# A scatter that waits for the scatter two places ahead of it, in a routed-experts kernel

## The chip, the cores and the metric

The kernel runs on one core of one Trainium2 chip. The metric is the device time of one execution in microseconds; three executions of the kernel before were timed, and their median is what the prediction is compared with. One more execution was recorded by the hardware profiler; every duration of a single instruction below comes from that recording.

The engines are called as in the profile: PE (matmuls), PEld (its weight loads), DVE (vector), ACT (scalar), POOL (GpSimd) and SP (which here only starts DMAs). SPq, POOLq and so on are the engines' queues.

## The reference

The input `x` has 16 rows of 512 tokens with 128 features. Each token is normalised to `xn`, and the result is

```
x + attention(xn) + experts(xn)
```

The attention is linear, with a decay: `scores[t, s] = (q[t]·k[s]) * d**(s-t-1)` for `s > t`, no softmax, with 32 features in q, k and v. The experts are four feed-forward networks; a router takes the two largest of four logits for each token, and only the two chosen results count:

```
logits = xn @ router_w + router_b + load_balancer
rw, sel = top_k(logits, 2);  rw = softmax(rw)
e0 = (silu(xn @ w1) * (xn @ w3)) @ w2          e1 = gelu(linear(xn) @ c1w + c1b) @ c2w + c2b
e2 = two layer norms around a relu network      e3 = gelu(xn @ ml_w1 + ml_b1) @ ml_w2 + ml_b2
out = x + attention + rw[0] * e_sel0 + rw[1] * e_sel1
```

All data are 32-bit floats.

## The kernel before

**First part: rows.** The 16 rows are loaded, normalised, transposed and projected. Four rows at a time (a "quad") go through the attention, are added to `x`, and are stored to the output by a plain DMA on SP. The rows are also gathered in six groups of 1, 1, 2, 4, 4 and 4 rows for the routing. For a group, `route` and `count` on DVE work out which pair of experts each token wants and which place in that pair's list it gets; there are six pairs, so six lists, all in one DRAM table called `lists`. Then the group's normalised tokens are written to their places. That is `Group.send`, one indirect DMA for each 128 tokens, issued by POOL. Each row of it has 131 floats: 128 features, two weights and the token's number, which lie in SBUF in a tile called `pay`. The places lie in a tile called `idx`, one column for each scatter. There are 64 such list scatters, named `send0.0` to `send5.15` in the plan.

**Second part: tiles.** The lists are read back in 21 tiles of two to four times 128 tokens (`TURN` gives the order: pair, number, and the group that must have been sent). A tile is loaded from `lists` into `xg` by SP (step `L`), transposed (`T`), pushed through the two experts of its pair, and summed in `o`: step `B` on DVE puts the biases into `o`, and the steps `J` on DVE add the experts' results. Then `Tile.send` adds `o` to the output, again by one indirect DMA for each 128 tokens, this time with accumulation in DRAM; the steps are called `X0` to `X3`. There are 66 of these output scatters. Their token numbers lie in a tile `to`, one column for each. There are four buffers for `o`, so `B` of a tile waits until the scatters of the tile four places ahead have landed.

**The order.** Each step is given to `add` with its engine, an estimated duration, the steps it follows, the buffers it takes and a rank. `emit` is a list scheduler over these: it keeps a time for each engine (`free`), works out when each ready step could start, picks the step that starts first (or a lower rank within 0.25 us of it), and calls its function, which writes the instructions. The order in which the functions are called is then the order on each engine, for PE, DVE, ACT and SP by a manual schedule, and for POOL by `queued`, which chains the instructions one behind the other. POOL is `G` in the plan. It has three kinds of work: the scatters, the powers `rstd_x`, `rstd_u` and `rstd_v` of the norms (`inverse`), and small copies and memsets.

Both kinds of scatter go through the helper `scatter`:

```
i = queued(nc.gpsimd.indirect_dma_start(
    out=o, out_offset=bass.IndirectOffsetOnAxis(ap=index, axis=0),
    in_=src, in_offset=None, bounds_check=n - 1, oob_is_err=False, **how,
), key)
```

In the plan a list scatter is a step of 1.28 us on POOL and an output scatter one of 1.87 us. Scatters post their completion to eight semaphores in turn, so before the change a scatter waits at most for the one eight places ahead of it.

At the very end there is a loop over rows that runs only if a list overflowed; it does not run with these inputs.

Of the kernel before, what the change touches and what calls it, by code (L numbers as in the profile page):

```python
# [83 lines left out]
def decay_attention__plus__routed_experts(  # L84
# [10 lines left out]
    nc = tc.nc  # L95
# [17 lines left out]
        "h2T": 1, "z2T": 1, "o": 4,  # L113
    }

    LATE = {"x": 3.0, "o": 3.2, "pay1": 2.6, "pay2": 2.6}


# [25 lines left out]
    def queued(i, key=None):  # L144

        if queue["on"]:
            others = [q for q, k in queue["moving"] if k != key or key is None]
            for q in others or [queue["fixed"]]:
                if q is not None:
                    tc.add_manual_dep(i.ins, q, behind, reason="the order of the plan")  # L150
            if key:
                queue["moving"].append((i.ins.name, key))
            else:
                queue.update(fixed=i.ins.name, moving=[])
        return i
# [7 lines left out]
    PE, V, A, G, S = "PVAGS"  # L163
# [7 lines left out]
    def emit():  # L171
        free = dict.fromkeys("PVAGS", 0.0)
        slots = {kind: [()] * n for kind, n in ROOM.items()}
        slots["x"] = [(f"store{b}",) for b in range(ROOM["x"])]
        done, left = {}, {n: len(p[3]) for n, p in plan.items()}
        followers = {}
        for n, p in plan.items():
            for q, _ in p[3]:
                followers.setdefault(q, []).append(n)
        ready = [n for n in plan if not left[n]]  # L180
        while ready:
            starts = {}
            for n in ready:
                eng, us, fn, after, takes, rank, at = plan[n]
                t = max(at, free[eng])
                for q, lat in after:
                    if lat is None:
                        lat = 0.05 if plan[q][0] == eng else 0.2
                    t = max(t, done[q] + lat)
                for kind in {k for k, _ in takes}:  # L190
                    ends = sorted(
                        max((done[q] for q in s), default=-1.0) + LATE.get(kind, 0.2)
                        for s in slots[kind] if all(q in done for q in s)
                    )
                    count = sum(k == kind for k, _ in takes)
                    t = max(t, ends[count - 1]) if len(ends) >= count else None
                    if t is None:
                        break
                if t is not None:
                    starts[n] = t  # L200
            assert starts, f"no step can go on: {ready}"
            first = min(starts, key=starts.get)
            eng, soon = plan[first][0], starts[first] + 0.25
            n = min(
                (m for m in starts if plan[m][0] == eng and starts[m] <= soon),
                key=lambda m: (plan[m][5], starts[m]),
            )
            eng, us, fn, after, takes, rank, at = plan[n]
            for kind, users in takes:
                i = min(  # L210
                    (i for i, s in enumerate(slots[kind]) if all(q in done for q in s)),
                    key=lambda i: max((done[q] for q in slots[kind][i]), default=-1.0),
                )
                slots[kind][i] = (n, *users)
                given.setdefault((kind, n), []).append(i)
            running[0] = n
            fn()
            running[0] = None
            done[n] = free[eng] = starts[n] + us
            ready.remove(n)  # L220
            for m in followers.get(n, ()):
                left[m] -= 1
                if not left[m]:
                    ready.append(m)
        assert len(done) == len(plan), "a step waits for itself"
# [253 lines left out]
    def transposed(z, n, name):  # L479
# [2 lines left out]
            nc.tensor.transpose(pt[:, ts(c, P)], z(c), ident)  # L482
        return pt[:, : n * P]

    def scatter(o, src, index, n, key, **how):

        i = queued(nc.gpsimd.indirect_dma_start(  # L487
            out=o, out_offset=bass.IndirectOffsetOnAxis(ap=index, axis=0),
            in_=src, in_offset=None, bounds_check=n - 1, oob_is_err=False, **how,
        ), key)  # L490
        tc.add_to_no_dep_group(key, i.ins)
        tc.declare_no_dep(i.ins, group=key, reason="each row of the table is written once at most")
        if key == "lists":
            tc.declare_no_dep(i.ins, group="loads", reason="a tile is loaded when all its rows are there")

    def chosen(lg, n, pool, name):

        cin = pool.tile([P, NL, 1 + n], F32, tag=f"cin{n}", name=f"cin_{name}")  # L500
        pair = cin[:, :, 1:]
        dif = pool.tile([P, NL, n], F32, tag=f"dif{n}", name=f"dif_{name}")
        firsts = [(e, NE - 1 - e, e * (2 * NE - 1 - e) // 2) for e in range(NE - 1)]
        for e, m, at in firsts:
            nc.vector.tensor_tensor(
                dif[:, at : at + m], lg[:, e : e + 1].to_broadcast([P, m, n]), lg[:, e + 1 :], ALU.subtract
            )

        won = pool.tile([P, NL, n], F32, tag=f"won{n}", name=f"won_{name}", bufs=1)
        nc.vector.tensor_scalar(won, dif, 0.0, 0.5, ALU.is_ge, ALU.subtract)  # L510

        sums = pool.tile([P, NE, n], F32, tag=f"sums{n}", name=f"sums_{name}", bufs=1)
        w = lambda l: won[:, l, :]
        nc.vector.tensor_tensor(sums[:, 1, :], w(3), w(4), ALU.add)
        nc.vector.tensor_tensor(sums[:, 2, :], w(5), w(3), ALU.subtract)
        nc.vector.scalar_tensor_tensor(sums[:, 3, :], w(4), -1.0, w(5), ALU.mult, ALU.subtract)
        nc.vector.tensor_reduce(sums[:, 0, :], won[:, : NE - 1].rearrange("p l c -> p c l"), AX.X, ALU.add)
        nc.vector.tensor_tensor(sums[:, 1:], sums[:, 1:], won[:, : NE - 1], ALU.subtract)
        for e, m, at in firsts:
            nc.vector.tensor_tensor(  # L520
                pair[:, at : at + m], sums[:, e : e + 1].to_broadcast([P, m, n]), sums[:, e + 1 :], ALU.add
            )
        nc.vector.tensor_scalar(pair, pair, 1.5, None, ALU.is_gt)
        return cin, dif
# [173 lines left out]
    class Group:  # L698
# [52 lines left out]
        def send(s, k):  # L751
            scatter(lists, s.entry(k), s.idx[:, k : k + 1], NL * LR, "lists")
# [30 lines left out]
    for g, m in enumerate(GROUPS):  # L783
# [41 lines left out]
        n = NC * m  # L825
# [19 lines left out]
    class Tile:  # L845
# [138 lines left out]
        def send(s, c):  # L984
            scatter(rows_of_out, s.o[:, c, :], s.to[:, c : c + 1], B * T, "out", compute_op=ALU.add)
# [69 lines left out]
    with tc.manual_schedule(engines={E.PE, E.DVE, E.Activation, E.SP}):  # L1055
        queue["on"] = True
        emit()
        queue["on"] = False
# [29 lines left out]
    with tc.For_i(0, trips, 1) as i:  # L1088
# [20 lines left out]
        s = Dense(0, 3, 0, NC, "row")  # L1109
# [90 lines left out]
```

## Time and profile before

| what | value |
|---|---|
| time, median of 3 | 320.58 us (319.81 to 322.14) |
| time of the profiled execution | 373.55 us |
| span of the profiled execution | 371.5 us |
| granted PE clock in it, mean | 0.891 |
| PE busy | 307.8 us (83%) |
| DVE busy | 208.7 us (56%) |
| POOL busy | 203.6 us (55%) |
| ACT busy | 160.1 us (43%) |
| list scatters on POOL | 64, mean 991 ns |
| output scatters on POOL | 66, mean 1561 ns |

The profiled execution is 53 us longer than the median of the timed ones. Its durations are those of single instructions, and sums of them are compared with its own time. [...] In a timeline line the columns are the start in us, the duration in us, engine, source line and operation, what is written and read, the number of instructions, and in brackets the idle time before with what ended it.

### The profile page before, as it was taken

The page shows a single profiled execution, that of the slowest core. Times are in us where ns is not written, and L with a number is a line of the kernel's source. Part 1 is how long each engine was busy: PE and PEld are TensorE (multiplying, and loading weights), DVE is VectorE, ACT ScalarE, POOL GpSimd, SP SyncE. Part 2 cuts the span into 40 slices and gives each one's busy share as a digit, 9 for nine tenths or more (in the row PEclk, how much of TensorE's full clock was granted, in tenths as well). Part 3 has the DMA queues.
Part 4 walks back from the last instruction along what each step waited for, and adds up shares of the span by engine and source line. Part 5 has one row for each costly group of instructions (what it writes and reads, how often), then busy time and mean ns, then how long its engine had stood idle before and what let it go on. Part 6 is the DMA issues. An engine that isn't in the chain of part 4 may idle for free. (4 is left out here: it accounts for less than half of the span.)

```text
span 371.5 us, 6510 instructions
## 1 busy us (share of the span) xinstructions
PE 307.8 (83%) x2194; PEld 234.0 (63%) x2194; DVE 208.7 (56%) x857; ACT 160.1 (43%) x358; POOL 203.6 (55%) x247
## 2 busy tenths in 40 slices
PE   1996979879300998996999999999999999999970
PEld 1854858455300695865468785775886877885860
DVE  4875657739230385731375964785858685475420
ACT  3784764336200613353253636144476266333420
POOL 5508773744775030277648884844364641784282
PEclk9986886668655599999899999999999999999995
DMA  7991174440251005021505362422133310442032
GB/s 225 283 205 50 39 211 117 119 119 8 78 167 43 1 17 156 9 75 36 79 8 66 28 89 21 66 21 36 12 55 58 43 16 1 69 48 19 3 33 23
DMA packets 34148, 25.60 MB, mean 69 GB/s; under 512 B 3648, under 2 KB 31552, under 8 KB 33984
## 3 DMA queue, kind: packets, MB, share of 16 engines
q0 software_dynamic: 11552, 8.50, 16.6%
q1 hardware_dynamic: 21840, 15.39, 16.4%
q10 hardware_dynamic: 720, 1.26, 1.0%
q8 instruction: 19, 0.31, 0.4%
q14 instruction: 17, 0.14, 0.1%
HBM read 11.65 MB, written 13.62 MB: 68 GB/s over the span
## 5 line engine op out<-in xcount | busy, mean ns | idle before, releaser
L487 POOL DMA_INDIRECT out_dram<-o,to x66 | 103.0, 1561 | 48.2 <-DVE o L939 33.1
L487 POOL DMA_INDIRECT lists<-pay,idx x64 | 63.4, 991 | 48.7 <-DVE sc L637 19.3
L939 DVE SCALAR_TENSOR_TENSOR o<-y_ps,xg,o 128x128 f32<-128x128 f32 x132 | 38.0, 345 | 51.7 <-PE y_ps L158 41.6
L158 PE MATMUL y_ps<-main_sb,h 128*128 128x128 f32 x456 | 55.4, 276 | 0.9 <-ACT h L916 0.9
L158 PEld LDWEIGHTS y_ps<-main_sb,h 128*128 128x128 f32 x456 | 53.7, 192 | 3.7 <-issue 1.2
L158 PE MATMUL proj_ps<-w_all,xnT 128*128 128x68 f32 x128 | 22.6, 344 | 19.3 <-ACT xnT L565 19.2
L158 PEld LDWEIGHTS proj_ps<-w_all,xnT 128*128 128x128 f32 x128 | 21.1, 254 | 21.0 <-ACT xnT L565 20.5
L158 PE MATMUL h_ps<-xT,main_sb 128*128 128x512 f32 (+2 forms) x88 | 34.1, 487 | 0.0
L916 ACT ACTIVATE h<-h_ps,cols_sb 128x512 f32<-128x512 f32 (+2 forms) x44 | 24.7, 579 | 17.2 <-PE h_ps L158 11.9
L902 DVE SCALAR_TENSOR_TENSOR th<-th,a_ps 128x384 f32<-128x384 f32 (+2 forms) x36 | 20.2, 566 | 18.8 <-ACT th L899 18.3
L158 PE MATMUL a_ps<-xT,w_sb 128*128 128x384 f32 (+2 forms) x72 | 29.9, 501 | 0.5 <-ACT xT L867 0.5
L916 ACT ACTIVATE h<-h_ps,b_e 128x512 f32<-128x512 f32 (+2 forms) x28 | 17.4, 626 | 29.7 <-PE h_ps L158 29.4
L158 PE MATMUL b_ps<-xT,w_sb 128*128 128x384 f32 (+2 forms) x72 | 28.5, 525 | 0.4 <-ACT xT L867 0.4
L899 ACT ACTIVATE th<-a_ps 128x384 f32<-128x384 f32 (+2 forms) x36 | 17.8, 499 | 24.9 <-PE a_ps L158 24.4
L475 ACT ACTIVATE pay<-x,off_x,rstd_x 128x128 f32<-128x128 f32 x64 | 26.1, 487 | 2.5 <-DVE off_x L470 2.5
L158 PEld LDWEIGHTS y_ps<-sw_w2h,h 128*128 128x128 f32 x224 | 26.1, 192 | 1.3 <-issue 0.5
L465 POOL TENSOR_TENSOR rstd_x<-ve_x,neg_half 128x4 f32<-128x4 f32 x16 | 16.4, 1030 | 18.9 <-DVE ve_x L460 15.2
L158 PE MATMUL y_ps<-sw_w2h,h 128*128 128x128 f32 x224 | 26.5, 275 | 0.0
L158 PE MATMUL h_ps<-xT,w_e 128*128 128x512 f32 (+2 forms) x56 | 25.2, 546 | 0.9 <-ACT xT L867 0.9
L465 POOL TENSOR_TENSOR rstd_u<-ve_u,neg_half 128x3 f32<-128x3 f32 (+2 forms) x8 | 8.2, 1022 | 28.2 <-DVE ve_u L460 28.2
L565 ACT COPY xnT<-xnT_ps 128x512 f32<-128x512 f32 x16 | 9.0, 583 | 32.8 <-remote 25.0
L907 DVE TENSOR_TENSOR h<-th,b_ps 128x384 f32<-128x384 f32 (+2 forms) x36 | 20.2, 568 | 2.2
(180 smaller groups left out, 506.5 us busy)
## 6 DMA issues: line engine op xcount, KB each, us to landing
x<-in_x_dram SPq DMA_DIRECT2D x16, 256.0 KB
out_dram<-x SPq DMA_DIRECT2D x16, 256.0 KB
xg<-lists SPq DMA_DIRECT2D x8, 262.0 KB
xg<-lists SPq DMA_DIRECT2D x8, 196.5 KB
main_sb<-in_main_dram SPq DMA_DIRECT2D x1, 1216.0 KB
out_dram<-o,to POOLq DMA_INDIRECT x66
lists<-pay,idx POOLq DMA_INDIRECT x64
lists<-none SPq DMA_DIRECT2D x6, 131.0 KB
```

The lines of the kernel that those rows point to most:

```text
L158: nc.tensor.matmul(o, lhsT, rhs, start=start, stop=stop)
L465: queued(nc.gpsimd.tensor_tensor(rstd, ve, neg_half[:, :n], ALU.pow))
L475: nc.scalar.activation(o(c), v(c), AF.Identity, bias=off[:, c : c + 1], scale=rstd[:, c : c + 1])
L487: i = queued(nc.gpsimd.indirect_dma_start(out=o, out_offset=bass.IndirectOffsetOnAxis(ap=index, axis=0), in_=src, in_offset=None, bounds_c ...
L565: nc.scalar.copy(s.xnT, s.bank)
L899: nc.scalar.activation(s.th[i], s.ga[i], AF.Tanh, scale=0.5)
L902: nc.vector.scalar_tensor_tensor(s.th[i], s.th[i], 1.0, s.ga[i], ALU.add, ALU.mult)
L907: nc.vector.tensor_tensor(s.h0[:, i, :], s.th[i], s.gb[i], ALU.mult)
L916: nc.scalar.activation(getattr(s, key)[:, i, :], s.hb[key, i], func, bias=bias[:, i : i + 1])
L939: nc.vector.scalar_tensor_tensor(o, s.py[e][:, c, :], w(c), o, ALU.mult, ALU.add)
```

## The change

`emit` now keeps, for the last two scatters, the time at which it expects each to have landed (`LANDS`: 2.45 us after the start of a list scatter, 3.45 us after that of an output scatter). A scatter is not planned to start before the older of the two has landed. If it would start less than 0.5 us after that, the plan puts a memset ahead of it. The memset overwrites the column of indices that the scatter two places ahead has read. As that column is still an input of that DMA, the memset has to wait for the DMA's semaphore, and the new scatter stands behind the memset in POOL's queue.

```diff
+    LANDS = {"s": 2.45, "X": 3.45}
...
+        landed = [0.0, 0.0]
...
                 t = max(at, free[eng])
+                if eng == G and n[0] in LANDS:
+                    t = max(t, landed[0])
...
+            if eng == G and n[0] in LANDS:
+                if starts[n] < landed[0] + 0.5:
+                    rest.append(indexes[-2])
+                landed = [landed[1], starts[n] + LANDS[n[0]]]
             running[0] = n
             fn()
...
+    indexes, rest = [], []
+
     def scatter(o, src, index, n, key, **how):
 
+        if rest:
+            queued(nc.gpsimd.memset(rest.pop(), 0))
         i = queued(nc.gpsimd.indirect_dma_start(
...
+        indexes.append(index)
```

In the built program 83 memsets are added, all on POOL: 45 ahead of list scatters (none in group 0, 2 of 4 in group 1, 5 of 8 in group 2, then 9, 16 and 12 of 16) and 38 ahead of output scatters. The order of instructions on PE, DVE, ACT and SP is the same as before, and so is the order of POOL's other work.

## The prediction

> **What bounds the kernel now.** I began with the page: busy shares, slices, then the groups of line 487, where all scatters are issued.
>
> ```profile
> PE 307.8 (83%) x2194; PEld 234.0 (63%) x2194; DVE 208.7 (56%) x857; ACT 160.1 (43%) x358; POOL 203.6 (55%) x247
> PE   1996979879300998996999999999999999999970
> POOL 5508773744775030277648884844364641784282
> L487 POOL DMA_INDIRECT out_dram<-o,to x66 | 103.0, 1561 | 48.2 <-DVE o L939 33.1
> L487 POOL DMA_INDIRECT lists<-pay,idx x64 | 63.4, 991 | 48.7 <-DVE sc L637 19.3
> ```
>
> A slice is 9.3 us. From slice 19 (176 us) to slice 37 PE is busy 90% or more: this part, the tiles, is bound by PE. Before it, rows, routing, list scatters and first tiles hand over to each other and PE pauses. POOL is busy 55%; before its output scatters it idles 48.2 us, mostly for DVE's sums. It is not the bound, except at the very end: PE's last slices are 7 and 0, POOL's are 8 and 2.
>
> Then the waits.
>
> ```profile
> SPq L857 <- DVE o L939: 174.0, 16, 28.9
> ACT xnT L565 <- remote: 25.0, 1, 25.0
> ```
>
> Loads from `lists` wait mostly for DVE to finish with an older tile's buffer, seldom for a scatter. The second line is a pause of ACT (95.5 to 120.5 us) that no engine's record explains; DVE has one of 6.4 us just before it, ACT one of 5.0 at 75.7, DVE one of 6.2 at 170. The profiled execution took 373.55 us (span 371.5 and 2 around it), 53 us over the median of 320.58, so timed runs can't contain all of these pauses. My sum is a difference from single durations: I add it to 373.55 for the profile and to 320.58 for the median, since none of its terms is a pause.
>
> **The price of a wait.** Removed: nothing. Added: 83 memsets on POOL, each with a wait. Nothing moves on another engine; no DMA is added. I need three numbers: the period of scatters, the time from start to landing, the time from landing to the next start.
>
> Period, from POOL's timeline:
>
> ```profile
> 98.64 0.97 POOL L487 DMA_INDIRECT lists<-pay,idx  x1 [0.30 <-issue]
> 99.91 0.97 POOL L487 DMA_INDIRECT lists<-pay,idx  x1 [0.30 <-issue]
> ...
> 361.70 1.54 POOL L487 DMA_INDIRECT out_dram<-o,to  x1 [0.30 <-DVEq L1088]
> 363.55 1.54 POOL L487 DMA_INDIRECT out_dram<-o,to  x1 [0.30 <-DMA out_dram<-o,to]
> ```
>
> List scatters start 1.28 us apart, output scatters 1.85; two places are 2.56 and 3.69.
>
> Landing of a list scatter: a load on SP issued right after the landing it waited for (timelines of POOL and SP).
>
> ```profile
> 155.74 1.04 POOL L487 DMA_INDIRECT lists<-pay,idx  x1 [0.20 <-issue]
> ...
> 158.29 0.34 SPq L857 DMA_DIRECT2D xg<-lists  x1
> ```
>
> So 2.55 us at most. The last output scatter, started at 363.55, moved its last packets in the stretch 366.4 to 366.7, and the waits that close the program end before the last of them starts:
>
> ```profile
> L1088 SPq EVENT_SEMAPHORE  x14: 17/28/3371, 361.3 to 367.3; - x14
> ```
>
> (columns: shortest, median, longest in ns, first and last start). Landing lies between 2.9 and 3.75 us; the list scatters' packets end 1.85 after the start, 0.7 before their landing, so I take 2.9 + 0.7 = 3.6.
>
> From landing to start: the trace has no memset between scatters, but a small copy there.
>
> ```profile
> 77.01 0.97 POOL L487 DMA_INDIRECT lists<-pay,idx  x1 [0.30 <-issue]
> 77.97 0.36 POOL L708 COPY pay<-tok 128x8 f32<-128x8 f32 x2
> 78.48 0.99 POOL L487 DMA_INDIRECT lists<-pay,idx  x1 [0.15 <-issue]
> ```
>
> The copy follows the scatter without a gap, and the next scatter comes 0.15 after it. A memset of 128x1 takes 0.10 in this trace, so memset and gap are 0.25 and replace the ordinary 0.30: **a memset whose semaphore has already come is free.** One that must wait costs landing + 0.28 (0.10, plus a gap between 0.15 and the 0.20 seen after other instructions). Two list places become 2.55 + 0.28 = 2.83, or 0.135 more for each scatter; two output places 3.6 + 0.28 = 3.88, or 0.095 each. The ends for output scatters: at 3.4 nothing, at 3.75 0.17.
>
> Here the Trainium skill stands against the row. Its page "DMA: Bandwidth & Descriptors", section "Anatomy of one DMA — SWDGE (gpsimd) path", gives about 2.0 us plus bytes over 436 GB/s; for 67 KB that is an estimate of 2.15 us for either kind. Then 2.15 + 0.28 is under 2.56 and far under 3.69, every semaphore has come, and the sum is zero. The rows say 2.55 and about 3.6, more for the accumulating one, and they decide: the waits bind, barely. The same page's "Rules for kernel authors" speak against the change: issue a DMA early and wait late, so that the fixed part overlaps. Here a part of 2 us that overlapped comes to stand in POOL's queue.
>
> **What of it is on the path.** In full: 45 × 0.135 = 6.1 us for lists, 38 × 0.095 = 3.6 for outputs, together 9.7.
>
> - *Tail.* The last eight scatters run from 350.61 with nothing beside them at the end; six have a memset. They gate in three pairs: 3 × (3.88 − 3.69) = **0.6 us**, fully on the path (ends: 0 and 1.0).
> - *Output scatters before.* Behind a waiting memset stand `rstd_u` and `rstd_v`, for which DVE, ACT and then PE wait. POOL mostly arrives first (it waited 28.2 us for `ve_u`, 14.2 for `ve_v`). Only between 190 and 228 does it run without idle time. Of 32 × 0.095 = 3.0 I take a sixth, **0.5**.
> - *Lists.* Behind them stand `rstd_x`, later the first output scatters. In groups 0 to 3 POOL waits for rows anyway (3.6, 1.65 and 9.0 us between 56 and 89 us). Groups 4 and 5 have 28 memsets, 3.8 us. Who is late next? DVE's `weigh` of group 5 waits for earlier scatters, and its `B` of the fifth tile for the first tile's output scatters. In the profile those have landed by 181.8 (178.19 + 3.6) and `B` runs at 191.4: 9.6 us of cover. Without the pauses PE and DVE come earlier and the cover shrinks. If it is gone all 3.8 count; I take a third, **1.3**.
>
> The sum is +2.4 us: 320.6 + 2.4 = **323.0**; for a profiled execution with the same pauses, 376.
>
> **Rivals.**
>
> *Slower: landings under load.* While x is stored and reloaded, SP's queue q1 fills the DMA engines. The group 2 scatter issued at 53.53 still had packets after 58.5, and the load behind it went out at 59.32: 5.8 us to land. Stretches 50.0 to 50.5 and 53.5 to 54.0:
>
> ```profile
> q1 hardware_dynamic: 274, 0.14, 99.6%
> q1 hardware_dynamic: 290, 0.15, 101.2%
> ```
>
> Before, POOL went on at 1.28 through this; with two in flight the period becomes (5.8 + 0.28)/2 = 3.0. Such load lay over scatters for some 11.5 us (48 to 53.5, 100 to 106): 9.0 scatters become 3.8, and 5.2 × 1.28 = 6.7 us are lost. With the 6.1 above the list phase ends 12.8 later. It decides once that exceeds the cover; with half of it left (4.8) 8.0 remain, with the tail 8.6: **329**. For it: the loads are in the trace, and stores come in bunches. Against: most fall where POOL is not yet the late one.
>
> *Faster: the pauses are the scatters' doing.* All four lie in runs of scatters issued back to back (70 to 79, 91 to 117, 155 to 183). If fewer in flight end them and timed runs contain a quarter of their 36 us (5.0, 92.9 to 120.5, 3.3 where two overlap), 9 to 10 us go: **311**. Against: at 2.55 us to land and one every 1.28, two are in flight already, and between 107 and 118 the software queue is empty between scatters. A cap at two changes little there, and 53 us of pauses are missing from timed runs.
>
> *It doesn't do what it says.* If scatters land sooner without the profiler (2.2 and 3.4 us are enough), each memset finds its semaphore set: **320.6**.
>
> **How the numbers follow.** Forecast 0.50, loaded landings 0.30, nothing 0.07, faster 0.13. About 1% (3.2 us) is what a measurement here can tell from no change. Of the forecast 0.09 spills over +1%, so slower has 0.39; same has 0.41 + 0.07 = 0.48; faster 0.13. The forecast's own range is 320.5 to 326. The range that should hold eight in ten, 317.5 to 330.5, takes in loaded landings; below it lies most of the faster case.
>
> **What would show it.** Right: starts two places apart of 2.8 in runs of list scatters and 3.8 to 3.9 in outputs; memsets with `DMA` as the releaser, 0.1 to 0.3 us each; PE still busy 90% from about 176 us on. Starts 2.56 and 3.69 apart would mean the waits never bind; several waits over 1 us beside stores, the loaded case; a missing pause at 95 us with a faster median, the third. Wrong altogether: a change over 10 us either way.

## The result, and the profile after

| | before | after |
|---|---|---|
| median of 4 | 321.36 us (319.81 to 323.04) | 358.67 us (357.79 to 361.57) |
| profiled execution | 373.55 us | 358.33 us |
| mean granted PE clock in it | 0.891 | 0.929 |

The ratio is 1.118 (95% interval 1.109 to 1.127). Here and below, times are medians of all runs, while ratios compare the means of the fast runs alone, those within 1.5% of the fastest of their kernel. The changed kernel is 37.3 us slower, where the forecast was 2.4 slower and the range ended at 330.5. In the two profiles the order is the other way round: the profiled execution of after is 15 us *shorter* than that of before.

The experiments below show where this oddity comes from, and it is needed to read every number: **the kernel before takes two different times.** On four of the six chips used for them it takes 373 to 375 us (medians of 7), with the pauses that its profile shows; on the other two it takes 322 us, and the profiles of changed kernels taken there have no such pauses. Each time all seven runs agreed. Only one chip was used on two occasions (373.9 and 373.6 us), so whether the pauses go with the chip or with the occasion is not shown. The timed runs of the comparison above agree with the shorter time, the profile of before with the longer. The changed kernel takes 358 us in the comparison on record and 358 us on a chip where the kernel before has pauses. So below, each ratio is against the kernel before timed beside it on the same chip, and "with pauses" or "without pauses" says what the kernel before did there.

The page of after: its PE and POOL rows of busy time and slices (a slice is now 8.9 us), and the two scatter groups.

```profile
PE 307.6 (86%) x2194; PEld 231.5 (65%) x2194; DVE 207.4 (58%) x857; ACT 160.3 (45%) x358; POOL 212.6 (60%) x330
PE   1998977797999667999989979899999999999930
POOL 4608665858555466768787757533737714683571
L501 POOL DMA_INDIRECT out_dram<-o,to x66 | 103.3, 1565 | 51.4 <-DVE o L954 28.4
L501 POOL DMA_INDIRECT lists<-pay,idx x64 | 63.2, 987 | 37.9 <-issue 15.6
```

The hole of before in slices 10 to 12 (PE 3, 0, 0) is gone. Instead PE is at 6 and 7 tenths in many slices of the first half, and once more at 7 in the tiles. The scatters themselves cost what they did, 0.99 and 1.57 us. Among the waits (total, times, longest):

```profile
POOL idx L500 <- DMA lists<-pay,idx: 17.1, 13, 2.5
DVE off_x L479 <- POOL rstd_x L474: 15.2, 9, 4.9
DVE off_u L479 <- POOL rstd_u L474: 11.0, 6, 6.0
POOL to L500 <- DMA out_dram<-o,to: 4.4, 7, 1.0
```

The first and fourth rows are the new waits. The second and third are what stood behind them. The same two in the profile of before:

```profile
DVE off_x L470 <- POOL rstd_x L465: 5.1, 3, 3.9
DVE off_u L470 <- POOL rstd_u L465: 1.5, 2, 0.9
```

No row names "remote" any more. SP's own waits, which stood at 174.0 us for `o` before, still come mostly from there, but the loads of tiles now wait long for list scatters too:

```profile
SPq L872 <- DVE o L954: 146.0, 13, 22.9
SPq L872 <- DMA lists<-pay,idx: 75.0, 6, 18.3
```

The second row was 20.2 us in the profile of before, and 52.6 in the one profile below in which list scatters run freely without pauses.

The price of a wait is read from POOL's timeline in group 4:

```profile
102.72 0.97 POOL L501 DMA_INDIRECT lists<-pay,idx  x1 [0.62 <-issue]
105.05 0.10 POOL L500 MEMSET idx<- 128x1 uint32 x1 [1.35 <-DMA lists<-pay,idx]
105.81 1.00 POOL L501 DMA_INDIRECT lists<-pay,idx  x1 [0.66 <-issue]
106.80 0.12 POOL L500 MEMSET idx<- 128x1 uint32 x1
107.11 0.97 POOL L501 DMA_INDIRECT lists<-pay,idx  x1 [0.19 <-issue]
```

A memset that has to wait ends, and 0.66 us pass before the scatter behind it starts ("issue": nothing in the profile is waited for). A memset that finds its semaphore set costs no more than the old gap: 0.12 and 0.19 where there were 0.30. So scatters go in pairs, one start after a wait, the next some 1.3 us later. From landing to start is 0.10 + 0.66 = **0.76 us, where the prediction had 0.28**.

At the end of the program, the last eight output scatters:

```profile
341.14 1.55 POOL L501 DMA_INDIRECT out_dram<-o,to  x1 [0.53 <-issue]
342.23 0.58 POOL L500 MEMSET to<- 128x1 uint32 x1
343.00 1.55 POOL L501 DMA_INDIRECT out_dram<-o,to  x1 [0.19 <-DVE any_over L1083]
344.41 0.26 POOL L500 MEMSET to<- 128x1 uint32 x1
345.24 1.55 POOL L501 DMA_INDIRECT out_dram<-o,to  x1 [0.57 <-issue]
347.50 0.10 POOL L500 MEMSET to<- 128x1 uint32 x1 [0.71 <-DMA out_dram<-o,to]
348.32 1.55 POOL L501 DMA_INDIRECT out_dram<-o,to  x1 [0.73 <-issue]
```

Here a memset's record begins inside that of the scatter ahead of it, so a wait seldom shows as idle time; the starts tell it. Two places are 4.10 us (341.14 to 345.24), and 5.32 for the last pair, where before had 3.69. The eight take 15.27 us from first to last start (333.05 to 348.32), before 12.94.

### The profile page after: what moved, and what is told of

Same layout as the page of the kernel before. It is cut to its first block, busy times and chain, and to the rows that moved or that the text cites. A ratio compares the mean times of both kernels' runs of the same rounds, so it can differ in the third digit from the quotient of the medians.

```text
span 356.3 us, 6536 instructions
## 1 busy us (share of the span) xinstructions
PE 307.6 (86%) x2194; PEld 231.5 (65%) x2194; DVE 207.4 (58%) x857; ACT 160.3 (45%) x358; POOL 212.6 (60%) x330
## 4 chain that ended last, share of the span: by engine, by line
PE 56%; POOL 18%; issue 10%; ACT 6%; DVE 5%; DMA 2%; POOLq 0%; SPq 0%; DVEq 0%
PE y_ps L160 19%; PE h_ps L160 9%; POOL out_dram L501 7%; POOL lists L501 5%; PE f_ps L160 5%; PE a_ps L160 4%; PE b_ps L160 4%; PE proj_ps L160 4%; PE xnT_ps L491 2%; POOL rstd_x L474 2%; ACT pay L484 2%; ACT z L484 2%; DMA x<-in_x_dram 2%; POOL rstd_u L474 1%; PE nt_ps L160 1%
## 5 line engine op out<-in xcount | busy, mean ns | idle before, releaser
L501 POOL DMA_INDIRECT lists<-pay,idx x64 | 63.2, 987 | 37.9 <-issue 15.6
L160 PE MATMUL h_ps<-xT,main_sb 128*128 128x512 f32 (+2 forms) x88 | 35.2, 501 | 0.0
L160 PE MATMUL h_ps<-xT,w_e 128*128 128x512 f32 (+2 forms) x56 | 26.6, 573 | 0.9 <-ACT xT L882 0.9
L160 PE MATMUL b_ps<-xT,w_sb 128*128 128x384 f32 (+2 forms) x72 | 26.8, 500 | 0.4 <-ACT xT L882 0.4
L160 PEld LDWEIGHTS proj_ps<-w_all,xnT 128*128 128x128 f32 x128 | 20.5, 248 | 2.4 <-ACT xnT L580 1.8
L922 DVE TENSOR_TENSOR h<-th,b_ps 128x384 f32<-128x384 f32 (+2 forms) x36 | 20.2, 568 | 2.2
L900 DVE TENSOR_SCALAR o<-rows_sb,xg 128x128 f32<-128x128 f32 x66 | 15.2, 294 | 9.1 <-DMA out_dram<-o,to 4.6
L160 PEld LDWEIGHTS h_ps<-xT,main_sb 128*128 128x128 f32 x88 | 15.9, 196 | 6.7 <-issue 2.6
L484 ACT ACTIVATE z<-uv,off_u,rstd_u 128x128 f32<-128x128 f32 x23 | 9.7, 484 | 21.3 <-DVE off_u L479 21.3
```

The source lines that it names most:

```text
L160: nc.tensor.matmul(o, lhsT, rhs, start=start, stop=stop)
L484: nc.scalar.activation(o(c), v(c), AF.Identity, bias=off[:, c : c + 1], scale=rstd[:, c : c + 1])
L501: i = queued(nc.gpsimd.indirect_dma_start(out=o, out_offset=bass.IndirectOffsetOnAxis(ap=index, axis=0), in_=src, in_offset=None, bounds_c ...
L900: nc.vector.tensor_scalar(o, bias, w(c), None, ALU.mult)
L922: nc.vector.tensor_tensor(s.h0[:, i, :], s.th[i], s.gb[i], ALU.mult)
```

## The experiments

### With pauses and without

The kernel before again, unchanged, on two chips, and the changed kernel on a third.

> The kernel before, unchanged, profiled once more. If the pauses of the first profile (25.0 us of ACT and others) belong to that one execution, this profile takes 320 to 325 us, has no idle time of ACT over 10 us with no releaser, and its first output scatter starts at about 125 to 135 us. If profiling always brings them, it takes about 370 us again.

> The changed kernel, timed beside the kernel before on one chip. The kernel before took 321 us where the change was first measured and 374 us in the last comparison. Theory A (the pauses of the other engines come or stay away with the place where a kernel runs, and the waits keep them away): about 358 us here whatever the kernel before takes; where the kernel before takes 374 the change is then 4% faster. Theory B (the change costs 37 us everywhere): about 411 us beside 374, or 358 beside 321.

> The kernel before, profiled again. Where it is timed at 321: a profile of 318 to 323 with no pause of ACT or DVE over 5 us put down to remote, list scatters still 1.28 us apart, the first output scatter at 124 to 131 us and the time from it to the last one 182 to 186 us (worked out from the other runs: lists 27.5 us shorter than in the changed kernel, outputs 9.7). Where it is timed at 374: the pauses again, first output scatter at 172 to 174 us.

| run | this | before beside it | ratio |
|---|---|---|---|
| before_again | 374.7 us (one run) | 374.4 us | |
| before_third | 374.3 us (one run) | 375.4 us | |
| after_again | 358.0 us | 373.2 us | 0.962 (0.954 to 0.970) |

On these chips the change makes the kernel 4% *faster*. The pauses are not an accident of one recording: they come in every profile of before, at nearly the same places. The rows of before_third:

```profile
ACT xnT L565 <- remote: 23.8, 1, 23.8
DVE x L696 <- remote: 15.7, 2, 12.1
ACT h L916 <- remote: 6.5, 1, 6.5
```

The assumption that timed runs could not contain these 53 us holds for the comparison on record and fails on these chips.

The granted clock differs as well: in timed runs of the kernel before it is 0.89 to 0.92 with pauses and 0.96 to 0.98 without. That these chips are slower as such does not explain the longer time: the kernel with list waits alone, below, takes the same time with and without pauses (348.9, 349.9 and 350.2 us) with profiled clocks of 0.938, 0.940 and 0.927.

### The two halves of the change

Waits for list scatters alone, or for output scatters alone. (The halves have 44 and 39 memsets, also in the whole change: the groups' counts 2, 5, 9, 16 and 12 add up to 44, not 45. The memset ahead of the very first output scatter overwrites a column of `idx`.)

```diff
-                if starts[n] < landed[0] + 0.5:
+                if n[0] == "s" and starts[n] < landed[0] + 0.5:     # list_only, list_second, list_third
+                if n[0] == "X" and starts[n] < landed[0] + 0.5:     # out_only, out_second, out_third
```

> Memsets ahead of list scatters only (44), none ahead of output scatters. Theory (POOL's list scatters come late, and the tiles and output scatters behind them): 345 to 355 us, most of the 37 us. Rival (output scatters, which are more delayed near the end of the kernel, carry the loss): 321 to 328 us.

> Memsets ahead of output scatters only (39), none ahead of list scatters. If the pauses come from runs of list scatters, they are back: beside a kernel before of 374 us this takes 372 to 380 us, and beside one of 321 us 321 to 328 us. If the output scatters carry the loss, 350 us or more beside 321.

> Waits for list scatters alone, timed again. Its list waits cost 27.5 us where before has no pauses: then ratio 1.075 to 1.095 (345 to 352) beside 321, against 1.004 by the prediction's term for lists. Where before takes 374: ratio 0.92 to 0.94 as the first time.

> Waits for output scatters alone, timed again. Where before takes 321: 328 to 334, ratio 1.02 to 1.04 (9.7 us), against 1.003 by the prediction's terms for outputs and tail. Where before takes 374: 1.01 to 1.03 as the first time.

> Waits for list scatters alone. Beside a kernel before of about 321: ratio 1.075 to 1.095 (27.5 us of the 37.3), against 1.004 by the prediction's term. If it comes out under 1.05, most of the 37.3 us are the output scatters' doing and the sum worked out across chips is wrong. Beside 374: 0.92 to 0.94, nothing new.

> Waits for output scatters alone. Beside 321: ratio 1.02 to 1.04 (9.7 us), against 1.003 by the prediction's terms for outputs and tail; its profile has no pauses and the first output scatter at 124 to 131 us. Beside 374: 1.01 to 1.02, nothing new.

| kernel | with pauses, first time | with pauses, second time | without pauses |
|---|---|---|---|
| lists alone | 348.9 us, 0.932 (0.924 to 0.941) | 349.9 us, 0.932 (0.929 to 0.936) | 350.2 us, **1.086** (1.081 to 1.092) |
| outputs alone | 378.5 us, 1.018 (1.009 to 1.027) | 380.6 us, 1.014 (1.010 to 1.017) | 333.0 us, **1.035** (1.030 to 1.040) |

Where there are no pauses, the list waits cost 28.0 us (350.15 − 322.12) and the output waits 10.9 (333.02 − 322.12). The sum is 38.9, against the 37.3 of the whole change. The first time, lists alone came out at the 345 to 355 us expected, but beside a kernel before of 374 us, where the range had supposed one of 321. The kernel with list waits takes the same on all three chips: it hardly has pauses to lose. Outputs alone also gives the one profile in which list scatters run freely without pauses. Its page, and that of lists alone beside it (both from the chip without pauses; first outputs alone, then lists alone):

```profile
PE   1998998899999999999897998999999999999920
POOL 4706886868777876886967575337377226871761
```

```profile
PE   1996989696999992999999999999999999999960
POOL 4607673866555457668888858533737713882382
```

With free list scatters (above) PE is at 8 or 9 from the second slice on through the first half, and POOL mostly at 6 to 8. With list waits (below) POOL falls to 4 or 5 in slices 10 to 14, and PE has slices at 6 and 2. The starts in POOL's timeline say how much of that reaches the end; the last column is what lies between the first and the last output scatter.

| kernel | mean period in group 4 | first output scatter | first to last output scatter |
|---|---|---|---|
| outputs alone, without pauses | 1.28 us | 127.9 us | 194.4 us |
| lists alone, without pauses | 1.97 us | 157.6 us | 182.9 us |
| after | 1.94 us | 155.0 us | 193.3 us |
| before, its own profile (with pauses) | 1.28 us | 172.6 us | 191.0 us |

(The period is the time from the group's first scatter to its last over 15.) A kernel before without pauses would start its outputs at 127.9 and take 182.9 to the last one, 7.9 to the end of the span and 2.1 around it: 320.8, where 322.1 was measured. The list waits put the first output scatter 29.7 us later, and the output waits stretch the last part by 11.5, of which 2.7 in the last eight scatters (15.6 for 12.9).

What ties the lists to the tiles shows best in group 5. In lists alone without pauses, between 128 and 160 us, the norms of the tiles stand behind waiting list scatters, and PE, which is at 2 in slice 15, waits for them:

```profile
DVE off_u L479 <- POOL rstd_u L474: 8.3, 1, 8.3
PE zuT_ps L491 <- ACT z L484: 6.9, 1, 6.9
```

### Is a memset without a wait free?

```diff
-                    rest.append(indexes[-2])
+                    rest.append(idle[:, :1])       # a tile that no DMA reads
```

> The same 83 memsets in the same places, but into a column that no DMA reads, so that they wait for no landing. Theory (the wait for the landing, and the scatter's own preparation that it exposes, cost the time): 320 to 324 us, starts of list scatters in runs still 1.28 us apart. Rival (an instruction between two scatters breaks their overlap, whatever it waits for): 340 us or more, starts 1.5 us or more apart.

368.8 us beside 374.4 (with pauses), ratio 0.983 (0.972 to 0.994). Both ranges expected supposed a kernel before of 321 us, so the starts decide. In group 4:

```profile
96.45 0.97 POOL L502 DMA_INDIRECT lists<-pay,idx  x1 [0.19 <-issue]
97.40 0.13 POOL L501 MEMSET idle<- 128x1 uint32 x1
97.72 0.97 POOL L502 DMA_INDIRECT lists<-pay,idx  x1 [0.19 <-issue]
```

List scatters still start 1.28 us apart, the last eight output scatters take 12.99 us for 12.94, and the long pauses are there. The 83 memsets move no start; the waits do. This kernel was not run without pauses.

### What the list phase is worth: one place back

```diff
-                    rest.append(indexes[-2])
+                    rest.append(indexes[-1])       # lists alone
```

> A list scatter waits for the one right ahead of it; output scatters do not wait. By what was measured (landing 2.6, then 0.76 to the next start) list scatters then start 3.3 to 3.4 us apart, group 4 takes 53 us instead of the 30 of the changed kernel, and group 5 stretches alike. Theory 'the list phase lies on the path': the first output scatter moves from 155 to 190 to 205 us and the end moves by as much, 380 to 400, ratio 1.01 to 1.08. Rival, that of the prediction, 'most of a list wait is covered': the end moves by less than a third of what the first output scatter moves, below 363. No long pause in either.

415.1 us beside 373.6 (with pauses), ratio 1.121 (1.105 to 1.137), slower than the range expected. The period in group 4 is 3.35 us as expected; the first output scatter comes at 223.2. From two places back (155.5 in list_only) to one that is 67.7 us, and the time grows by 66.2 (348.9 to 415.1, on two chips with pauses). Between first and last output scatter hardly anything changes (182.9 after 183.7). So **the list phase of POOL lies on the path in full** once list scatters wait, and no cover is seen. The waits:

```profile
POOL idx L500 <- DMA lists<-pay,idx: 78.4, 44, 4.5
DVE off_x L479 <- POOL rstd_x L474: 32.2, 10, 12.2
DVE to L886 <- DMA xg<-lists: 25.3, 3, 21.2
```

All 44 memsets wait, and the norms of the rows and the tiles wait behind them.

### Do the waits end the pauses, or does the spacing?

First the strength of the wait: three places back instead of two, for all scatters and for lists alone; and two places back for the lists of groups 0 to 3 (early) or 4 and 5 (late) alone.

```diff
+                    rest.append(indexes[-3])                        # three_back; lists_three: lists alone
-                if starts[n] < landed[0] + 0.5:
+                if n[0] == "s" and int(n[4:n.index(".")]) < 4 and starts[n] < landed[0] + 0.5:   # early_lists; "> 3" in late_lists
```

> Each memset overwrites the column of the scatter three places ahead, not two, so three scatters may be in flight. Theory: a landing of 2.55 plus 0.76 from landing to start is 3.3 us, below three periods of 3.84, so only loaded landings are waited for: 322 to 332 us. Rival (any wait for a landing on POOL costs the same): 350 to 358 us.

> A list scatter waits for the one three places ahead; output scatters do not wait. With everything three back the time was 359.1, and an unbound memset ahead of an output scatter starts inside the record of the scatter before it and moves no start. So if output memsets that find their semaphore set are free: the same as with all three back, ratio to before 0.945 to 0.965, and remaining pauses of up to 7 us. If they cost: below 355, ratio under 0.945. With two back for lists alone the ratio was 0.932; three back should be no better, since the pauses return as more is in flight.

> Memsets ahead of the list scatters of groups 0 to 3 only (16). Beside a kernel before of about 374 us: the 25 us pause stays and the short one over group 3 goes, 366 to 374 us. Beside a kernel before of about 321 us: 323 to 335 us.

> Memsets ahead of the list scatters of groups 4 and 5 only (28). Beside a kernel before of about 374 us: if the pauses come from many list scatters in flight, the 25 us pause of ACT, which lies over group 4, goes, and the time is 345 to 356 us; the pause of about 5 us over group 3 stays. Beside a kernel before of about 321 us: the loss of the waits alone in these groups, 330 to 345 us.

| kernel (with pauses) | time | ratio | largest pauses in its profile |
|---|---|---|---|
| three_back | 359.1 us | 0.953 (0.942 to 0.965) | 6.9, 6.9, 4.6 us |
| lists_three | 363.7 us | 0.981 (0.967 to 0.996) | 16.0, 7.5, 5.2 |
| early_lists | 361.5 us | 0.963 (0.950 to 0.975) | 10.3 in two, 9.4, 9.3 |
| late_lists | 354.4 us | 0.946 (0.933 to 0.959) | 5.1, 3.8, 3.3 |

Each takes part of the pauses away, and none as many as waits two places back on all lists. The ranges for three_back supposed a kernel before of 321 us; 359.1 lies just outside the rival's and confirms neither. In three_back 4 memsets are shown waiting for a list scatter, in lists_three 3. lists_three fell short of its expectation in either form: its ratio is worse than that of three_back, which ran on another chip. In early_lists the pause of ACT over group 4 did not stay whole, as expected, but came as two of 9.4 us, and the time fell below the range. late_lists came out as expected. How much of the pauses stays depends on more than the number in flight; on what else is open.

Then the spacing without a wait. The memset fills a private tile of N columns; it takes POOL's time and waits for no DMA. Output scatters are as before.

```diff
-                    rest.append(indexes[-2])
+                    rest.append(idle)              # lists alone; idle is 128 x N
```

> The 44 list scatters that got a memset in the changed kernel get one here too, but it fills a private tile of 128x704 and waits for no DMA: about 0.7 us of POOL's time, so that list scatters start some 1.9 us apart, as the waits space them in group 4 of the changed kernel. Output scatters are as before the change. Theory 'spacing' (pauses come from too many scatters in flight, whatever keeps them apart): no pause of ACT or DVE over 7 us, first output scatter at 150 to 160 us, time 344 to 354, ratio to before 0.92 to 0.945. Rival 'it takes the wait itself': the pause of ACT of 24 to 25 us stays and the time is 366 to 376, ratio 0.98 to 1.01.

> The same with a fill of 128x320, about 0.4 us, so that list scatters start some 1.5 to 1.6 us apart instead of 1.28 (before) and 1.9. Spacing: some of the pauses stay and are shorter, 352 to 366. The wait itself: 366 to 376 with the long pause.

> The fill without a wait, between the two sizes tried: 128x512, about 0.53 us, so that list scatters start 1.65 to 1.7 us apart. Spacing: the pauses are gone or under 5 us and the first output scatter comes earlier than with 1.84 (149.6), at 140 to 147 us; time 336 to 343. If the threshold lies above 1.7, pauses of 5 to 15 us are left and the time is 344 to 350. The kernel before beside it: 368 to 377 if its pauses come on every occasion after the recorded comparison, about 321 if that state returns; in the latter this kernel must be slower than before, by 15 to 22 us, since the spacing alone then moves the list phase by 44 times 0.4.

| kernel | N | period in group 4 | first output scatter | time | before beside it |
|---|---|---|---|---|---|
| paced | 704 | 1.85 us | 149.6 us | 343.7 us | 373.6, ratio 0.927 (0.918 to 0.936) |
| paced_light | 320 | 1.52 us | 150.8 us | 346.5 us (340.6 to 348.3) | 373.6, ratio of the medians 0.927 |
| paced_mid | 512 | 1.68 us | 141.1 us | 335.6 us | 321.9, ratio 1.043 (1.034 to 1.051) |

The timeline of paced in group 4:

```profile
99.07 0.97 POOL L502 DMA_INDIRECT lists<-pay,idx  x1 [0.17 <-issue]
100.03 0.70 POOL L501 MEMSET idle<- 128x704 uint32 x1
100.90 0.97 POOL L502 DMA_INDIRECT lists<-pay,idx  x1 [0.16 <-issue]
```

No wait, and no pause left: its profile has no row with "remote". paced_light still has some; the two rows with the most:

```profile
ACT rT L704 <- remote: 14.8, 1, 14.8
ACT S L677 <- remote: 5.3, 2, 2.8
```

So on a chip with pauses the spacing is enough; the wait itself is not needed. paced has the lowest median measured with pauses, and it beats both kernels there. It is not told apart from paced_light (two of whose runs took 340.6 and 345.1 us), nor, by the ratios, from lists alone (0.932). paced came out just under the range expected, paced_light well under it (352 to 366). paced_mid met a chip without pauses, where spacing only costs: 13.6 us, of the 44 × 0.40 = 17.6 that its fills add, and a little less than expected. Its first output scatter comes 13.2 us later than the 127.9 of outputs alone, so the list phase lies on the path in full without pauses too. Whether it would have pauses on one of the other chips was not seen. Without pauses neither the change, nor its halves, nor paced_mid beats the kernel before.

The same timeline shows one thing more. Behind a fill of 0.70 us the scatter follows after 0.16; behind a memset of 0.10 that had waited it follows after 0.66. That fits a preparation of the scatter of some 0.6 to 0.8 us that runs while POOL is still busy with the instruction ahead, and that is laid bare when POOL has been standing still. It is an inference from these gaps; the trace has no record of the preparation.

## Why the prediction was wrong

**Landing to start (0.28 us).** The step "the copy follows the scatter without a gap, and the next scatter comes 0.15 after it" was measured behind an instruction that had *not* waited. Behind one that had, the gap is 0.66 us. A pair of list scatters that land in time then takes about 2.55 + 0.76 = 3.31, not 2.83. In lists alone (without pauses) four such pairs of group 4 took 3.69, 3.36, 3.16 and 3.39 us, 3.40 on average. That alone is (3.40 − 2.56) / 2 = 0.42 us for each scatter where the sum had 0.135.

**Landing (2.55 us) under load.** The rival was right that loaded landings come, and they are half of all: of the 19 list waits of lists alone, 9 ended 2.4 to 2.9 us after the start of the scatter waited for, and 10 later, up to 5.3. Its cause is seen once in group 4, in the stretch 120 to 123 us of lists alone, where a store of `x` fills the DMA engines (`q1` carries the stores and loads that SP starts, `q0` the scatters' data):

```profile
q1 hardware_dynamic: 1723, 0.92, 100.4%
q0 software_dynamic: 58, 0.13, 11.5%
```

The scatter of 118.30 landed after 4.69 us there. The rival missed a second cause. The wait that ended at 109.48 was for the scatter issued at 105.72, and SP's queue was silent. In the stretch 107 to 108 (`q8` carries loads of instructions):

```profile
q0 software_dynamic: 30, 0.06, 18.5%
q8 instruction: 1, 0.02, 7.1%
```

One packet of an instruction load holds one of the 16 DMA engines for 1.1 us (7.1% of 16 × 1 us). The scatter ahead of it, started at 103.63, moved its 32 packets together in 105 to 106. Of this one 30 moved between 107.2 and 107.6, and one moved alone in the stretch 108.3 to 108.4, when the load had ended; the wait ended 1.1 us after that, and the scatter is listed with 3.7 us from issue to landing. That fits a landing that comes with the slowest engine. The Trainium skill says so (page "DMA: Bandwidth & Descriptors", section "Why a DMA increments its semaphore by 16 and not by 1"): every engine posts its own increment, and only all 16 mean that the data are there. Of the 4.53 us of this pair some 1.1 are the load's. The wait that ended at 117.54 also has such a packet ahead of it: 30 packets of its scatter moved up to 115.3, the load's beside them.

In all, 7.3 us of waiting and 3.9 us of longer gaps stretch group 4 in lists alone by 11.2 us from its first scatter to the first of group 5 (31.64 us, against 16 × 1.28 = 20.5). The sum had 16 × 0.135 = 2.2.

**The cover ("I take a third").** "POOL waits for rows anyway" in groups 0 to 3 and "9.6 us of cover" behind groups 4 and 5 were read in a profile whose pauses had made everyone but POOL late. Without them POOL is late itself: half of the loss, 14.6 us, is there when group 4 begins (98.67 in lists alone, 84.12 in outputs alone). The waits between 40 and 98 us, first with list waits, then without:

```profile
POOL idx L500 <- DMA lists<-pay,idx: 11.3, 8, 2.6
DVE off_x L479 <- POOL rstd_x L474: 10.2, 4, 4.2
ACT pay L484 <- DVE off_x L479: 7.2, 3, 3.8
```

```profile
ACT pay L484 <- DVE off_x L479: 2.7, 3, 1.8
DVE off_x L479 <- POOL rstd_x L474: 0.6, 1, 0.6
```

`rstd_x` stands behind waiting scatters, the rows' norms wait for it, and `pay`, the source of the next scatters, waits for the norms. So these rows fit a loss that feeds itself. Named in the prediction ("Behind them stand `rstd_x` …"), it was then costed by a share instead of a chain; that `rstd_u` and `rstd_v` also stand behind the lists' waits, as in group 5 above, was left out. Lists: 1.3 expected, 28.0 measured.

Price and cover both failed, and they multiply. With the prediction's price and no cover at all, the lists would have come to its own 6.1 us. With the price of group 4 (11.2 / 16 = 0.70 for each scatter) 44 scatters come to an estimated 31, and the 28.0 measured are nearly all of that. So the forecast price was a fifth of the real one, and only a fifth of its sum (1.3 of 6.1) was put on the path, where nearly all of it lay. Mending one of the two alone leaves most of the miss.

**Outputs (0.5) and tail (0.6).** Landing was taken as 3.6 and measured at about 4: the seven waits of after ended 3.8 to 4.5 us after the start of the scatter waited for. With the gap of 0.66 to 0.73 behind a wait, two places take about 4.1 and not 3.88. The tail lost 2.3 in after and 2.7 in outputs alone, for 0.6. Before the tail the last part lost 8.8 us in outputs alone, for 0.5. PE waits there for the norms: in the 90 us after the first output scatter its weight loads waited 5.2 us for `z` with output waits,

```profile
PEld zvT_ps L491 <- ACT z L484: 5.2, 7, 2.9
```

against 0.7 without. Again the chain was named and then cut to a sixth. The remaining part of the 8.8 was not traced instruction by instruction.

**The pauses.** The rival "the pauses are the scatters' doing" was put aside because "a cap at two changes little there" and because timed runs do not contain them. Where the kernel before has pauses both reasons were wrong: its timed runs contain them, spacing the list scatters or a cap at two on lists takes them away and gains 7%, and the change itself gains 4%. In the timed runs that decided the comparison there was nothing to take away. Why chips or occasions differ, and what a burst of scatters does to ACT and DVE where there are pauses, stays open; no run here shows it. That the comparison on record was timed without pauses is known only by its times.

**What was right.** A memset whose semaphore has come is free. The waits bind, against the fit of the Trainium skill (2.15 us, sum zero): the shortest landing that was waited for took 2.4. The rule of its "Rules for kernel authors", issue early and wait late, spoke against the change, and going against it cost 37 us where there were no pauses. With pauses the change gained, so there the rule alone did not decide. The sign named for the faster rival, a missing pause with a faster median, is met on chips with pauses alone.

## What to carry to other kernels

A wait in front of a scatter that POOL issues costs more than the landing: add the longer gap behind the wait, here 0.66 us instead of 0.2, and count the slow landings too (here half of those waited for; one stray packet was enough), not only an undisturbed one. When work that others need stands in the same queue behind the wait, follow it until it comes back to the waiting queue, as `rstd_x` → norms → `pay` → next scatter does, before giving it a share; and don't read cover from a profile that holds pauses the timed runs lack. If scatters must be thinned out where bursts of them go with pauses, a fixed spacing did it at a ratio of 0.927 to the kernel before, waits on lists alone at 0.932, waits on all scatters at 0.962.

## What the runs showed of the hardware

- **Pauses.** The same program takes 322 us on two chips and 373 to 375 on four. With the longer time go pauses of ACT and DVE of up to 25 us, most of them during runs of list scatters 1.28 us apart. At 1.52 us one of 14.8 us and some of up to 2.8 are left, at 1.85 none. Their cause is open.
- **The gap behind a wait.** The gap ahead of a scatter is 0.16 to 0.23 us behind a memset or fill that had not waited, and mostly 0.66 to 0.75 behind a memset that had.
- **Instruction loads.** One packet of an instruction load on one of 16 DMA engines, 1.1 us long, went with a landing of a scatter after 3.7 us instead of some 2.5, its remaining data moving when the load had ended.
